# A graph layer on one core: nodes laid 49 to a partition, sources by rounding, the packed list stored in halves

## The chip, the core and the metric

The kernel runs on one core of a Trainium2 chip. The core has TensorE (PE, with PEld for its weight loads), VectorE (DVE), ScalarE (ACT), GpSimd (POOL) and SyncE (SP), each with a queue of its own that it works off in order; 16 DMA engines move data. The metric is the device time of one execution in microseconds, as a median over runs.

## The reference

A graph has 6250 nodes with 64 features and 206250 edges, sorted by their target node `dst`. What is computed:

```python
h = jnp.maximum(_layernorm(x, axis=-1), 0.0)
msg = h[src] + edge_attr_64                      # one row per edge
agg = jax.ops.segment_sum(msg, dst, num_segments=6250)
out = x + (jax.nn.relu(agg @ W1 + b1) @ W2 + b2)
```

W1 is 64x128, W2 is 128x64, all in float32.

## The kernel before

The edges' own rows and the source nodes' rows are summed separately.

Most edges have the sum over `h[src]` done by TensorE as a product. For a window of 252 target nodes a matrix of counts is built (how often does node s send to node d), by comparing lists of keys with ramps (`count`, L704: DVE makes `hot_lo` and `hot_key`, PE multiplies them to `pc`, ACT writes `pc` to `counts`), and then `counts` is multiplied with `h` in three bf16 parts (`product`, L750). There are 310 steps of `count`; a step n has extra work given to it in the dictionary `before` (L894). The edges' own rows come in chunks by SP (`feat`), and are summed against one-hot matrices (`chunk_sum`, L400).

The last 24 groups of 1024 edges (GP) are done otherwise: POOL gathers the source rows from a table of `h` in DRAM and adds them onto the edges' rows in SBUF (`pfeat`, 8 gathers of 128 rows a group, 192 in all), and two groups at a time are summed (`features_h`, L859). When a pair of groups is summed is decided while the program is written out, by a planner that counts 2.2 us a gather and 1.38 us a step.

The order of every engine's work is written by hand (`manual_schedule`). All gathers stand in POOL's queue: `rows` (15), `words` (15 and one for a second list), `dstq` (5) and `pfeat`.

The stretch before step 0, the prologue, does this:

- SP loads `firsts_i` and then x in three thirds of 128 partitions (L151). Node n lies in partition n % 128, so a partition's rows are 256 B runs, 32 KB apart. The last 106 nodes come in a load of their own (L152).
- ACT's queue loads src (L140). ACT turns src to float (L242), and its queue loads dstn, the targets (L243). PE transposes the sources, ACT stores them as `srcl` (`turn_src`, L245).
- From `firsts` DVE and PE find in which row of 256 edges each node's list begins (`row_i`, L259); POOL fetches these rows (`fetch_row`, L275), ACT counts in them where the list begins (`seek`, L279), DVE makes an index of it (`place`, L285).
- DVE packs target and source in one word, (dst << 13) | src (L561), for two halves. One store from ACT's queue writes the list `packed` to DRAM (L564). From there POOL fetches each node's list (`fetch_pair`, L541, tile `words`), and `unpack` and `turn` (L587, L600) make keys of it.
- The layernorm is done by thirds: means (L463), centring and squares (L470, L473), variances (L478), `norm_scale` (L484), and `norm_h` (L492), which stores a third of the table from SP and copies `h` to bf16.
- `chunk_starts`, `chunk_rows`, `chunk_columns`, `chunk_index` (L303 to L339) find where each chunk's edges begin; the gather `dstq` (`fetch_dst`, L344) needs their `cols_i`, and so do the `feat` loads.

Since a node lies at row (n % 128) * 49 + n // 128 of the table, `table_rows` (L521) turns sources into rows by three integer operations, for the `pfeat` gathers.

After the loop come the last two pairs of groups and the rest of the products and the MLP; at step 99 the index of a second, short list is made (`second_n`, L661), for which POOL has one gather of `words`.

Of the kernel before, what the change touches and what calls it, by code (L numbers as in the profile page):

```python
# [9 lines left out]
F32 = mybir.dt.float32  # L10
BF16 = mybir.dt.bfloat16
# [96 lines left out]
def gnn_kernel(ctx: ExitStack, tc: tile.TileContext, x, src_t, dst_t, dst_g, edge, w1, b1, w2, b2, out):  # L108
# [31 lines left out]
    nc.scalar.dma_start(src, src_t[:, :GA * J])  # L140
    dstn = pr.tile([QA, 2, P * J], I32, name="dstn")

    firstp_i = small.tile([1, GP], I32, name="firstp_i")
    nc.scalar.dma_start(firstp_i.rearrange("o (q h k) -> o q h k", h=2, k=1),
                        dst_g[GA // 2:G // 2, :, 0:1].unsqueeze(0))
    xl = consts.tile([P, HI + 1, D], F32, tag="x", name="xl")
    nc.gpsimd.memset(xl[:, HI - 1, :], 0.0)
    thirds = [(0, 16), (16, 32), (32, HI)]
    for h0, h1 in thirds:
        h1 = min(h1, HI - 1)  # L150
        nc.sync.dma_start(xl[:, h0:h1, :], x[h0 * P:h1 * P, :].rearrange("(h l) d -> l h d", l=P))  # L151
    nc.sync.dma_start(xl[:N % P, HI - 1, :], x[N - N % P:, :])  # L152

# [59 lines left out]
    for q in range(JQ):  # L213
# [37 lines left out]
    turn_src(0)  # L251
    pf = ps.tile([P, IC], F32, tag="po", name="pf", bufs=1)
# [22 lines left out]
    def fetch_row(i):  # L275
        rows_of[i] = small.tile([P, L1], I32, name="rows", bufs=4)
        gather(rows_of[i], dst_g.rearrange("q h (r k) -> (q h r) k", k=L1), row_i[:, i:i + 1])

    def seek(i0, n):  # L279
        for i in range(i0, i0 + n):  # L280

            inrow = small.tile([P, L1], BF16, name="inrow", bufs=2)
            nc.scalar.activation(inrow, rows_of[i], AF.Sign, bias=nhalf[:, i:i + 1], accum_out=first[:, i, 1:2])  # L283
# [236 lines left out]

    def table_rows(index, tmp):  # L521

        nc.vector.tensor_scalar(tmp, index, LO_BITS, None, op0=OP.logical_shift_right)
        nc.vector.tensor_scalar(index, index, P - 1, None, op0=OP.bitwise_and)
        nc.vector.scalar_tensor_tensor(index, index, float(HI), tmp, op0=OP.mult, op1=OP.add)

    def find_groups():
# [31 lines left out]
    norm_means()  # L559
    for h in range(2):  # L560
        nc.vector.scalar_tensor_tensor(dstn[:, h], dstn[:, h], DST_BITS,  # L561
                                       srcl[:QA, h].rearrange("q p j -> q (p j)"),
                                       op0=OP.logical_shift_left, op1=OP.bitwise_or)
# [12 lines left out]
    place(3, 4)  # L576
    fetch_pair(2)
    norm_var(2)
# [290 lines left out]
    chunk_starts(0, 2 * RC, "pc", 2)  # L869
    src_hi = late.tile([P, NWIN + NX], BF16, tag="part", name="src_hi").bitcast(I32)[:, :GP * J]  # L870
# [12 lines left out]
    load(1)  # L883
# [7 lines left out]
    def then(k, f):  # L891
# [193 lines left out]
    with tc.If(odd > 0):  # L1085
# [20 lines left out]
        with tc.For_i(0, G, 1) as g:  # L1106
# [6 lines left out]
            nc.sync.dma_start(index, src_t[:, ds(g * J, J)])  # L1113
            index_hi = work.tile([P, J], I32, name="index_hi", bufs=1)
            table_rows(index, index_hi)
            dst_1 = work.tile([P, J], I32, name="dst_1", bufs=1)
# [61 lines left out]
```

## Time and profile before

| | |
|---|---|
| median of 3 runs | 522.75 us (520.2, 522.75, 527.85) |
| profiled execution, its own time | 525.21 us |
| its span, first to last instruction | 523.4 us |
| granted TensorE clock, mean | 0.974 |
| DMA moved | 78.78 MB, 151 GB/s over the span |
| step 0, first count on PE | at 42.9 us |
| first `dstq` gather on POOL | at 37.6 us |
| last `pfeat` gather on POOL | at 503.0 us |

The page gives busy time of each engine, a chain of work that ended last, and groups of instructions by line with what ended the idle time before them. In a timeline the columns are start, duration, engine, line, operation, output<-input, shapes, how many, and in brackets the idle time before it and what ended that. A time of several equal instructions in a row is merged to one line.

### The profile page before, as it was taken

What the parts mean: (1) busy time and instruction counts of PE and PEld (TensorE: products, weight loads), DVE (VectorE), ACT (ScalarE), POOL (GpSimd) and SP (SyncE); (2) the same over time, 40 slices, a digit from 0 to 9 for tenths busy, and PEclk for the clock granted to TensorE, in tenths of its full rate; (3) what the DMA queues carried; (4) which work ended last, traced back from release to release, by engine and by line L of the source; (5) the groups of instructions that cost most, each with busy time, mean ns of one, the idle gap of its engine ahead of it and who ended that gap; (6) DMA issues with size and microseconds to landing.
All of it is one profiled execution on the core that took longest, in us unless ns stands there. A gap on an engine that the chain in (4) does not pass through costs nothing. (4 is left out here: it accounts for less than half of the span.)

```text
span 523.4 us, 19099 instructions
## 1 busy us (share of the span) xinstructions
PE 451.5 (86%) x8183; PEld 385.6 (74%) x8184; DVE 417.4 (80%) x618; ACT 360.1 (69%) x534; POOL 415.7 (79%) x265
## 2 busy tenths in 40 slices
PE   3026767999699999988999999999999999999954
PEld 3015555888588888777888888888888888888743
DVE  5589986889699989988898978888879888879210
ACT  5246898778467767896777777777777777768300
POOL 6358888888888868888889888888888888888840
PEclk9999899999799999999999999999999999999977
DMA  9819812566577766654666676676577676676610
GB/s 203 211 42 329 220 29 39 146 172 156 117 171 179 167 171 181 171 138 95 161 162 155 149 178 153 140 184 163 129 173 175 137 198 146 141 192 164 155 14 14
DMA packets 118152, 78.78 MB, mean 151 GB/s; under 512 B 39096, under 2 KB 113326, under 8 KB 117870
## 3 DMA queue, kind: packets, MB, share of 16 engines
q1 hardware_dynamic: 88458, 64.95, 42.7%
q0 software_dynamic: 29200, 10.25, 16.7%
q10 hardware_dynamic: 404, 2.30, 1.5%
q8 instruction: 66, 1.08, 0.9%
q14 instruction: 24, 0.20, 0.1%
HBM read 73.48 MB, written 3.99 MB: 148 GB/s over the span
## 5 line engine op out<-in xcount | busy, mean ns | idle before, releaser
L267 POOL DMA_INDIRECT pfeat<-table,src_p x192 | 363.5, 1893 | 58.5 <-issue 54.9
L722 ACT ACTIVATE counts<-pc 128x882 bf16<-128x882 f32 x310 | 276.8, 908 | 41.0 <-PE pc L720 27.0
L720 PE MATMUL pc<-hot_key,hot_lo 128*128 128x147 bf16 x1860 | 175.1, 231 | 24.2 <-DVE hot_key L712 17.5
L712 DVE TENSOR_TENSOR hot_lo<-iota_lo,keys 128x1536 bf16<-128x1536 bf16 x155 | 148.0, 955 | 46.5 <-PE pc L720 46.0
L720 PEld LDWEIGHTS <-hot_lo 128*128 128x128 bf16 x1860 | 135.3, 100 | 47.7 <-DVE hot_key L712 22.3
L712 DVE TENSOR_TENSOR hot_key<-iota_key,keys 128x1776 bf16<-128x1776 bf16 x155 | 167.1, 1078 | 0.0
L755 PE MATMUL pv<-counts,h 128*128 128x252 bf16 (+1 forms) x1078 | 149.6, 273 | 0.1
L755 PEld LDWEIGHTS <-h 128*128 128x128 bf16 x1078 | 99.2, 98 | 8.7 <-issue 0.4
L758 PE MATMUL pv<-counts,h 128*64 128x252 bf16 (+1 forms) x1078 | 78.0, 280 | 0.0
L407 PE MATMUL bank<-feat,hot 128*21 128x64 f32 x3168 | 59.0, 223 | 1.5 <-DMA feat<-in_edge 0.8
L410 ACT ACTIVATE by_node<-bank 128x128 f32<-128x128 f32 x66 | 18.4, 278 | 60.8 <-PE bank L407 60.7
L758 PEld LDWEIGHTS <-h 128*64 128x64 bf16 x1078 | 55.3, 113 | 4.4 <-issue 0.8
L407 PEld LDWEIGHTS bank<-feat,hot 128*21 128x21 f32 x3168 | 47.4, 102 | 14.8 <-issue 9.5
L395 DVE TENSOR_TENSOR hot<-rel,iota 128x504 f32<-128x504 bf16 x66 | 44.6, 677 | 0.6 <-PE bank L407 0.6
L267 POOL DMA_INDIRECT rows<-in_dst_g,row_i x15 | 18.6, 1238 | 14.9 <-ACT inrow L283 7.9
L267 POOL DMA_INDIRECT words<-packed,first_i x15 | 19.5, 1302 | 4.6 <-issue 3.4
L419 PE MATMUL pv<-select,by_node 128*64 128x42 f32 x264 | 21.2, 244 | 0.4 <-ACT by_node L410 0.4
L419 PEld LDWEIGHTS pv<-select,by_node 128*64 128x64 f32 x264 | 13.2, 137 | 9.1 <-issue 1.1
L440 PE MATMUL bank<-hotp,pfeat 128*64 128x42 f32 x384 | 14.7, 233 | 5.5 <-DMA pfeat<-table,src_p 4.2
L440 PEld LDWEIGHTS bank<-hotp,pfeat 128*64 128x64 f32 x384 | 12.8, 138 | 8.3 <-DMA pfeat<-table,src_p 4.7
L767 DVE TENSOR_TENSOR sums<-sums,pv 128x252 f32<-128x252 f32 x22 | 9.0, 409 | 10.9 <-PE pv L758 10.9
L309 PE MATMUL pstart<-begins,first 128*1 128x9 f32 (+2 forms) x30 | 1.2, 172 | 19.0 <-DVE first L287 19.0
(171 smaller groups left out, 273.5 us busy)
## 6 DMA issues: line engine op xcount, KB each, us to landing
feat<-in_edge SPq DMA_DIRECT2D x132, 384.0 KB
pfeat<-in_edge SPq DMA_DIRECT2D x24, 256.0 KB
pfeat<-table,src_p POOLq DMA_INDIRECT x192
xl<-in_x SPq DMA_DIRECT2D x3, 512.0 KB
out_y<-y SPq DMA_DIRECT2D x24, 63.0 KB
xs<-in_x SPq DMA_DIRECT2D x4, 315.0 KB
table<-xl SPq DMA_DIRECT2D x2, 512.0 KB
dstn<-in_dst_g ACTq DMA_DIRECT2D x1, 768.0 KB
```

The costliest lines, as they stand in the source:

```text
L267: nc.gpsimd.indirect_dma_start(out=rows, out_offset=None, in_=source, in_offset=bass.IndirectOffsetOnAxis(ap=index, axis=0), compute_op=op)
L395: nc.vector.tensor_tensor(hot_of[u][:, :n].rearrange("p c j w -> p (c j) w"), rel[:, c:c + n].rearrange("p c q k -> p (c q k)").unsqueeze( ...
L407: nc.tensor.matmul(bank[q * QP:q * QP + WQ, i * D:(i + 1) * D], hot[:, i, j, :], feat[i][:, j, :], start=(k == 0), stop=(k == JP - 1))
L410: nc.scalar.activation(by_node[u][:, :n].rearrange("p c d -> p (c d)"), bank[:, :n * D], AF.Copy)
L419: nc.tensor.matmul(pvs[b][0][i * D:(i + 1) * D, a:a + CN], of[:, i, :], select, start=False, stop=False)
L440: nc.tensor.matmul(pa[k:k + D, b, :], tiles[b][:, j, :], hot[:, j, :], start=(j < 2), stop=(j >= J - 2))
L712: nc.vector.tensor_tensor(hot.rearrange("p t (m o) -> p t m o", o=2), iota_k.rearrange("p (m o) -> p m o", o=2).unsqueeze(1).to_broadcast( ...
L720: nc.tensor.matmul(pc[:, k, m * K:(m + 1) * K], hot_lo[:, j, :], hot_key[:, j, :K], start=True, stop=True)
L722: nc.scalar.activation(counts[b % 2][:, :, s * ST * V:(s + 1) * ST * V].rearrange("p h (k m) -> p h k m", k=2), pc[:, :, :ST // 2 * K].rea ...
L755: nc.tensor.matmul(pv, h3[:, h, :2 * D], of, start=(h == 0 and not clear), stop=False)
L758: nc.tensor.matmul(pv[k:k + D, :], h3[:, h, 2 * D:], of, start=False, stop=(h >= HI - 2))
L767: nc.vector.tensor_tensor(at[:, :BN], at[:, :BN], pv[:, o:], op=OP.add)
```

## The change

Node n now lies in partition n // 49, so a partition holds 49 nodes that are neighbours in DRAM, and the table's row of node n is n itself. x comes as 112 partitions in three thirds (runs of 16 or 17 rows of 256 B), 15 partitions whole, and one partition with the last 27 nodes; the places without a node are zeroed first. `table_rows` is gone. The number that is packed for a source still has the partition-wise form, which is now 128 * (s % 49) + s // 49 where before s itself served; so s // 49 is found by scaling, adding and subtracting a large number, and the rest by one combining operation. dstn is loaded behind src at once. Packing is done by halves between the centrings, and each half is stored from SP. Seeks, fetches and places are regrouped: the first pair's words are unpacked after `norm_h`, the rows 7 to 10 are fetched behind `dstq`, and their seeks come at steps 4 and 5 instead of 15 and 16.

```diff
+    nc.scalar.dma_start(dstn, dst_g[:QA])          # behind src's load
...
-    nc.gpsimd.memset(xl[:, HI - 1, :], 0.0)
+    NL = N // HI                                   # 127
     thirds = [(0, 16), (16, 32), (32, HI)]
+    nc.gpsimd.memset(xl[96:, N % HI:, :], 0.0)
     for h0, h1 in thirds:
-        h1 = min(h1, HI - 1)
-        nc.sync.dma_start(xl[:, h0:h1, :], x[h0 * P:h1 * P, :].rearrange("(h l) d -> l h d", l=P))
-    nc.sync.dma_start(xl[:N % P, HI - 1, :], x[N - N % P:, :])
+        nc.sync.dma_start(xl[:112, h0:h1, :], x[:112 * HI, :].rearrange("(l h) d -> l h d", l=112)[:, h0:h1, :])
+    nc.sync.dma_start(xl[112:NL, :HI, :], x[112 * HI:NL * HI, :].rearrange("(l h) d -> l h d", l=NL - 112))
+    nc.sync.dma_start(xl[NL:, :N % HI, :], x[NL * HI:, :].unsqueeze(0))
...
+    lo_f = counts[0].rearrange("p h n -> p (h n)").bitcast(F32)[:, HI * D:HI * D + GA * J]
+    nc.scalar.activation(lo_f, src, AF.Copy, scale=1.0 / HI, bias=-(HI // 2) / HI)
     srcf = src.bitcast(F32)
-    nc.scalar.activation(srcf, src, AF.Copy)
-    nc.scalar.dma_start(dstn, dst_g[:QA])
+    nc.scalar.activation(srcf, src, AF.Copy, scale=float(P))
+    nc.vector.tensor_scalar(lo_f, lo_f, 1.5 * (1 << 23), 1.5 * (1 << 23), op0=OP.add, op1=OP.subtract)
...
-    turn_src(0)                                    # ahead of the products of pf
...
     for i in range(4):
         fetch_row(i)
+    nc.vector.scalar_tensor_tensor(srcf, lo_f, 1.0 - P * HI, srcf, op0=OP.mult, op1=OP.add)
+    turn_src(0)
     turn_src(1)
...
-    for h in range(2):
+    def pack(h):
         nc.vector.scalar_tensor_tensor(dstn[:, h], ...)
-    nc.scalar.dma_start(packed.rearrange("(q k) o -> q (k o)", q=QA), dstn.rearrange("q h k -> q (h k)"))
-    seek(0, 3)
-    for i in range(4, 7):
-        fetch_row(i)
-    place(0, 3)
+        nc.sync.dma_start(packed.rearrange("(q h k) o -> q h (k o)", q=QA, h=2)[:, h], dstn[:, h])
+    pack(0)
+    seek(0, 2)
+    fetch_row(4)
+    fetch_row(5)
+    norm_center(0)
+    pack(1)
+    seek(2, 2)
+    fetch_row(6)
+    norm_center(1)
+    place(0, 2)
     fetch_pair(0)
-    for k in range(3):
-        norm_center(k)
-        if k < 2:
-            seek(3 + 2 * k, 2)
+    norm_center(2)
+    seek(4, 3)
     norm_var(0)
     norm_var(1)
-    place(3, 4)
-    fetch_pair(2)
+    place(2, 5)
     norm_var(2)
...
-    table_rows(src_p, src_hi)
-    unpack_pair(0)
     chunk_rows(0, 2 * RC)
     chunk_columns(0, 2, "pc", 2)
-    turn_pair(0)
     norm_scale()
     chunk_index(0, 2)
     fetch_dst(0)
+    for i in range(7, 11):
+        fetch_row(i)
+    fetch_pair(2)
     fetch_pair(4)
     for k in range(3):
         norm_h(k)
+    unpack_pair(0)
+    turn_pair(0)
...
-        3: [lambda: open_pv(0, True), lambda: rows_later(7, 11)],
-        16: [lambda: seek(9, 2), lambda: rows_later(11, IC)],
-        18: [lambda: place(7, 4)],
+        3: [lambda: open_pv(0, True)],
+        4: [lambda: seek(7, 2)],
+        5: [lambda: seek(9, 2), lambda: rows_later(11, IC)],
+        8: [lambda: place(7, 4)],
-        15: [lambda: seek(7, 2), find_groups, lambda: norm_c(0), lambda: clear(0, 5)],
+        15: [find_groups, lambda: norm_c(0), lambda: clear(0, 5)],
```

The lists that come out differ also in this: with four rows fewer in the planner's queue, the pairs of `pfeat` groups are summed 3 to 6 steps earlier in the loop, the first at step 41 instead of 47; the last two pairs stay behind the loop in both. On POOL 53 `pfeat` gathers now stand ahead of the second list's words, 51 before.

More of the change, by code (lines that the diff above doesn't have):

```diff
@@ L146, in gnn_kernel @@
     xl = consts.tile([P, HI + 1, D], F32, tag="x", name="xl")
-    nc.gpsimd.memset(xl[:, HI - 1, :], 0.0)
+    NL = N // HI
+    assert NL == P - 1
     thirds = [(0, 16), (16, 32), (32, HI)]
+    nc.gpsimd.memset(xl[96:, N % HI:, :], 0.0)
     for h0, h1 in thirds:
-        h1 = min(h1, HI - 1)
-        nc.sync.dma_start(xl[:, h0:h1, :], x[h0 * P:h1 * P, :].rearrange("(h l) d -> l h d", l=P))
-    nc.sync.dma_start(xl[:N % P, HI - 1, :], x[N - N % P:, :])
+        nc.sync.dma_start(xl[:112, h0:h1, :], x[:112 * HI, :].rearrange("(l h) d -> l h d", l=112)[:, h0:h1, :])
+    nc.sync.dma_start(xl[112:NL, :HI, :], x[112 * HI:NL * HI, :].rearrange("(l h) d -> l h d", l=NL - 112))
+    nc.sync.dma_start(xl[NL:, :N % HI, :], x[NL * HI:, :].unsqueeze(0))
     zero = small.tile([P, 1], F32, name="zero")
@@ L519, in gnn_kernel @@
     nc.sync.dma_start(dst_p, dst_t.rearrange("p (g j) -> p g j", j=J)[:, GA:, :])
[L521 to L525, printed above, removed]
     def find_groups():
@@ L869, in gnn_kernel @@
     chunk_starts(0, 2 * RC, "pc", 2)
-    src_hi = late.tile([P, NWIN + NX], BF16, tag="part", name="src_hi").bitcast(I32)[:, :GP * J]
-    table_rows(src_p, src_hi)
-    unpack_pair(0)
     chunk_rows(0, 2 * RC)
     chunk_columns(0, 2, "pc", 2)
-    turn_pair(0)
     norm_scale()
@@ L1113, in gnn_kernel @@
             nc.sync.dma_start(index, src_t[:, ds(g * J, J)])
-            index_hi = work.tile([P, J], I32, name="index_hi", bufs=1)
-            table_rows(index, index_hi)
             dst_1 = work.tile([P, J], I32, name="dst_1", bufs=1)
```

## The prediction

> **What bounds the kernel now.** I read the page's busy shares first, then the chain that ended last in order of time, then the waits of POOL, and then the timelines of the two places these point to: the prologue and the neighbourhood of 190 us.
>
> ```profile
> PE 451.5 (86%) x8183; PEld 385.6 (74%) x8184; DVE 417.4 (80%) x618; ACT 360.1 (69%) x534; POOL 415.7 (79%) x265
> ```
>
> No engine is full, so the share decides nothing. The chain at the end does:
>
> ```profile
> 501.17 1.55 POOL pfeat L267
> 502.72 0.30 issue
> 503.03 3.56 DMA pfeat<-table,src_p
> 506.59 0.04 issue
> 506.63 0.45 PE bank L440 x2
> ```
>
> PE stands idle for the last `pfeat` gathers of POOL. By the timeline the last pair of groups (L440) would have been summed at about 501.9 with its data there, and was at 507.07: 5.2 us of slack on PE. What sets POOL's end? Its waits:
>
> ```profile
> POOL pfeat L267 <- issue: 54.9, 180, 0.3
> POOL rows L267 <- ACT inrow L283: 7.9, 1, 7.9
> POOL dstq L267 <- DVE cols L339: 4.5, 1, 4.5
> POOL words L267 <- DVE second_n L661: 3.8, 1, 3.8
> POOL rows L267 <- DVE row_i L259: 3.1, 1, 3.1
> ```
>
> The reader is to see that from the `dstq` gather on POOL waits for others only once, 3.85 us for `second_n`, a result of the counting loop. All else is 0.3 us between one gather and the next. POOL's end is therefore the start of `dstq`, plus a fixed list of gathers, plus that one wait. The prologue that leads to `dstq`, and to the loop:
>
> ```profile
> 19.09 2.35 DVE L561 SCALAR_TENSOR_TENSOR dstn<-dstn,srcl 96x1024 int32<-96x1024 int32 x2
> 21.85 0.51 ACT L283 ACTIVATE inrow<-rows,nhalf 128x256 bf16<-128x256 int32 x1 [8.80 <-DVE dstn L561]
> 22.71 0.95 POOL L267 DMA_INDIRECT rows<-in_dst_g,row_i  x1 [7.90 <-ACT inrow L283]
> 23.97 1.80 POOL L267 DMA_INDIRECT rows<-in_dst_g,row_i  x1 [0.30 <-issue]
> 26.07 2.04 POOL L267 DMA_INDIRECT rows<-in_dst_g,row_i  x1 [0.31 <-ACT counts L473]
> 28.42 0.95 POOL L267 DMA_INDIRECT words<-packed,first_i  x1 [0.30 <-DVE stat L478]
> 30.01 0.51 ACT L283 ACTIVATE inrow<-rows,nhalf 128x256 bf16<-128x256 int32 x1 [1.54 <-DMA rows<-in_dst_g,row_i]
> 37.64 1.82 POOL L267 DMA_INDIRECT dstq<-in_dst_g,cols_i  x1 [4.53 <-DVE cols L339]
> ```
>
> The chain: the last third of x is used at 17.67, after 2.71 us of waiting; then `pack` on DVE; the store of `packed` stands in ACT's queue, so ACT idles 8.80 us until the pack is done before it can seek; rows 4 to 6 are fetched only then; their last seek at 30.01 leads to `cols` and `dstq`. The loop's first count follows at 42.89.
>
> **The change, part by part.**
>
> *Loads.* src, dstn and x are 0.73 + 0.79 + 1.60 = 3.12 MB. x now comes in runs of 4 KB where it came in 256 B. The DMA view of the first 20 us, in half microseconds, shows both kinds:
>
> ```profile
> GB/s 0 0 0 68 57 171 376 433 331 94 264 225 216 218 216 368 211 287 236 270 237 202 157 189 219 216 219 217 218 237 261 321 282 332 108 107 191 296 270 188
> ```
>
> From 3 to 4.5 us, with src's 5.6 KB runs in flight, 331 to 433; later, mostly short runs, some 215. From 2.3 us on, 3.12 MB end at 10.5 (at 380) or at 16.8 (at 215). The new runs are nearer to the first row, so I take 12. SP's issue of the three thirds (6.22 us before, 5.14 more for the remainder) falls away; the five loads need no more than the table stores' 0.33 us each. The longer zeroing of `xl` on POOL (1472 columns; 0.15 us for 64 and 0.21 for 128 make 1.5) lies in POOL's 3.1 us wait for `row_i`; without that cover it would cost 1.5.
>
> *Sources by rounding.* ACT converts twice, 1.39 us each (L242): from 5.2 to 8.0. DVE rounds 128x1424: bounds 0.87 (the slope from 15 columns, 0.17 us, to 256, 0.29) and 1.69 (L561's kind, 1.22 for 1024); I take 0.9, the same operation's row. It lies in DVE's 0.98 us wait for `pf`; without it `row_i` is late by as much. If src lands later than 6.8, the rounding holds `row_i` up too; rows 0 and 1 are needed at 18 and land near 14, so some 3 us are covered. Then on the path: the combining operation, 1.69, from 9.9 to 11.6; three small ones to 12.2; the reductions 1.22 + 1.22 + 1.29 and L466 to 16.2. Meanwhile PE turns (2.0 each) from 11.6, and ACT stores `srcl` (2.1 each) at 15.7 and 17.8, `row2` at 18.0. `firstp_i` stands behind dstn now and must land by 11.6; it is 0.1 KB.
>
> *Packing in halves, stores on SP.* DVE: pack, center, pack, center (1.22 each) to 21.0, place 0.35, center, two variances to 24.9. ACT is free at 18.0, not at 21.85: seeks 0 and 1 to 19.0, square, seeks 2 and 3 to 21.1, squares to 23.7. POOL: row 4 at 18.6, 5 at 20.7, 6 at 22.8. Both first ones are beside DVE operations of two inputs, so 1.8 us each as at 23.97, not 0.95; row 6 lands at 25.7 (before, 28.11 to 30.01). Seek 6 and place end at 26.7, the last variance at 28.0. From L481 to `dstq` were 4.68 us; `table_rows` (0.86) and the unpacking (0.87) are gone from them: 2.95. **`dstq` starts at 31.0, 6.6 us earlier.** The halves' store, issued at 19.8, must land by then less two gathers; before it took at most 6.9 us (21.48 to 28.42), which would be 26.7 and still covered. On SP the first half's store waits for pack 0 (17.4), the second for pack 1 (19.8). Behind them stand two `pfeat` loads, not touched until about 47, and the table's stores, not ready before 32; so nothing on SP is late. Moving dstn's load to the front costs ACT 0.34 us of issue before src has landed.
>
> The rows' new place costs: gathers took 1.80 and 2.04 us beside L470, 0.95 beside the reductions. The sum has the slow ones; with 0.95 throughout, `dstq` would come 1.3 us earlier. The Trainium skill (SBUF — State Buffer, "Who interferes with whom") has a rule that speaks against this place: a DVE operation with two SBUF inputs contends with GpSimd instructions that read SBUF, a reduction on this chip never does; by it the sum is the one made here, without it the gain would be 1.3 us more.
>
> *POOL's list.* Two words gathers move from the idle prologue behind `dstq`, and four rows come under the norm_h operations. Bounds: 2 x 1.25 = 2.5 to 2 x 2.33 = 4.7 (the slowest words row, 2.03 + 0.3); I take 3.2, since some of them run clear. Besides, 53 instead of 51 `pfeat` gathers (2.2 us with its gap) stand ahead of the `second_n` words, so 2 fewer follow. POOL arrives there at 187.9 - 6.6 + 3.2 + 4.4 = 188.9.
>
> ```profile
> 191.74 0.90 POOL L267 DMA_INDIRECT words<-packed,second_i  x1 [3.85 <-DVE second_n L661]
> ```
>
> If the loop gains 2.9 us or more by then, nothing is waited for: POOL ends 6.6 - 3.2 + 3.85 = **7.25 us earlier**.
>
> *The loop.* The unpacking and turning of pair 0 come after norm_h. norm_h ends at 34.3, ACT's three h copies at 35.4, `klo` 0.42, transposes 1.1, keys 1.0, two hot operations 2.0: first count at 40.0, so 2.8 us earlier, and the 0.47 us wait for `dstq` goes. Unpacking used to be hidden; now DVE is idle about 2.8 us before the loop. Four seeks move from steps 15 and 16 to 4 and 5:
>
> ```profile
> 44.00:48.00 4.00, 2.94 (x20) 2.21 (x19) 4.00 (x5) 2.65 (x4) 3.39 (x3) 1.00 0.96 290
> ...
> 64.00:68.00 4.00, 2.64 (x28) 2.10 (x28) 3.38 (x4) 4.00 (x8) 3.69 (x2) 1.00 0.30 55
> ```
>
> Columns: stretch, its length, busy PE, PEld, DVE, ACT, POOL, clock. At 64 ACT is full (4.00 of 4), at 44 it is not (2.65) and DVE is. The seeks took 0.99 + 0.98 us there, so 0 to 2.0; I take 1.2. The loop gains 2.8 + 0.4 + 1.2 = 4.4, above the 2.9 needed. PE could end 4.4 + 5.2 = 9.6 us earlier, more than POOL's 7.25, so POOL decides.
>
> *The sum.* The profiled execution took 525.2 (span 523.4, 1.8 around it): 525.2 - 7.25 = 518.0. It lies 2.5 above the median of the runs shown, 522.75; on that footing 515.5. With x landing at 16.8, `dstq` starts 4.4 later and the gain is 2.85: 519.9. With fast gathers (6.6 + 1.3 - 2.5 + 3.85) it is 9.25: 513.5.
>
> **The rivals.** *The loop doesn't start earlier.* If the keys come late, behind norm_h and the copies, the loop keeps its 42.89, and `second_n` its 191.4. POOL then gains only the two gathers that no longer follow, 4.4 us: 518.4. For it: DVE idles before the loop. Against: 2.8 us of margin.
>
> *The tail of x.* Partitions 112 to 127 come in two loads of 15 and 1 long rows, and the first reduction waits for both besides its own third. At a sixteenth of 380 GB/s, 195 KB take 8.2 us; begun at 12, they end at 20.2, so the reductions start 7.9 late and `dstq` at 38.9, 1.3 later than now. With 3.2 more on POOL and 3.85 absorbed the end is 0.65 later: 523.4, slower. It decides from a first reduction later than 12.3 + 7.25 = 19.5. For it: no row here shows so few long rows. Against: 15 rows are not one.
>
> *More than the sum.* If the gathers at the loop's start also run clear of the burst at 40 to 52 us (290 to 379 GB/s in the windows), and of DVE, POOL's seven gathers from 37.64 to 50.0 fall from 1.46 to 0.95 each, 3.6 more, and the seeks give all 2.0: PE's 9.6 + 0.8 then decides, 512.3. For it: rows and words did go in 0.95 where they ran alone. Against: DVE has no pause there.
>
> **How the numbers follow.** Forecast 0.57 (513.5 to 519.9), loop or less than intended 0.18, tail 0.09, more 0.16. Time 515.5; 512.0 to 522.0 leaves out most of the tail and the far side of the last case. 2% is about what a measurement of this kernel can tell from no change, 10.5 us. Faster by that: half of the last case, which lies on the bound, and, since the three runs shown spread from 520.2 to 527.85, a quarter of the forecast: 0.08 + 0.16 = 0.24. Slower by that needs a tail far worse than priced: 0.05.
>
> **What would show it.** In the profile of after: the first `stat<-xl` reduction near 12.3; ACT without the 8.8 us wait; `dstq` near 31; the first count near 40; no wait at the second words; POOL's last gather near 497, PE still waiting briefly for it. A first reduction after 17, a count after 42, or a POOL wait that is new between 50 and 500 would make the prediction wrong.

## The result, and the profile after

The changed kernel takes 538.7 us (median of 4 runs, 537.42 to 539.5), the kernel before 524.16 beside it: a ratio of 1.028, with a 95% interval of 1.0228 to 1.0331. It is slower, where 515.5 and no measurable change were forecast. The profiled execution took 538.0 (span 536.1), against 525.21 (span 523.4). The granted TensorE clock, 0.934 in it against 0.974 before, does not explain this: two of the four runs had 0.96 and took 539.4 and 539.5.

The shares of the page have hardly moved. POOL has 13 us more than before, in as many instructions:

```profile
PE 452.4 (84%) x8183; PEld 386.4 (72%) x8184; DVE 417.8 (78%) x617; ACT 361.0 (67%) x535; POOL 428.9 (80%) x265
```

The chain that ended last (start, duration, what) still runs over POOL's last gathers; the last of them starts at 516.63, 13.6 us later than before (503.03):

```profile
514.77 1.55 POOL pfeat L274
516.32 0.30 issue
516.63 3.69 DMA pfeat<-table,src_p
```

POOL's waits (total, times, longest) show what moved:

```profile
POOL dstq L274 <- DVE cols L346: 6.5, 1, 6.5
POOL words L274 <- DVE second_n L669: 5.9, 1, 5.9
POOL rows L274 <- DVE nhalf L271: 5.2, 1, 5.2
...
POOL rows L274 <- ACT inrow L290: 2.2, 2, 1.9
```

The 7.9 us wait for the seek is gone as intended, but the waits for the row numbers (3.1 before), for `cols` (4.5) and for `second_n` (3.8) have each grown by about 2 us. Some rows of the prologue from the timeline, each with its start, its duration and the idle time before it:

```profile
9.35 0.17 DVE L232 CAST firsts<-firsts_i 128x8 f32<-128x8 int32 x1 [5.50 <-DMA firsts_i<-in_dst_g]
16.97 3.54 DVE L470 TENSOR_REDUCE stat<-xl 128x16 f32<-128x1024 f32 x3 [1.75 <-DMA xl<-in_x]
20.63 0.51 ACT L290 ACTIVATE inrow<-rows,nhalf 128x256 bf16<-128x256 int32 x1
21.49 3.46 POOL L274 DMA_INDIRECT rows<-in_dst_g,row_i  x1 [1.94 <-ACT inrow L290]
31.45 0.51 ACT L290 ACTIVATE inrow<-rows,nhalf 128x256 bf16<-128x256 int32 x1 [0.64 <-DMA rows<-in_dst_g,row_i]
36.63 1.82 POOL L274 DMA_INDIRECT dstq<-in_dst_g,cols_i  x1 [6.50 <-DVE cols L346]
```

x is there at 16.97, the last seek runs at 31.45, and `dstq` starts 1.0 us earlier than before, not 6.6. The rate of the DMA in the first 20 us, in half microseconds, says why x is late: 365 to 410 GB/s only from 3 to 4.5 us, then 330 and 295 and after that mostly 230 to 285.

```profile
GB/s 0 0 0 80 80 216 365 410 375 330 295 230 279 246 174 141 255 238 270 270 262 239 263 285 244 343 265 88 59 48 48 33 9 252 45 80 138 316 242 139
```

POOL's rows near 65 us hold the longest gather of the run. It is one of the four `rows` gathers of the last slabs, which took 0.94 to 1.54 us before:

```profile
64.87 1.54 POOL L274 DMA_INDIRECT rows<-in_dst_g,row_i  x1 [0.30 <-issue]
66.71 9.50 POOL L274 DMA_INDIRECT rows<-in_dst_g,row_i  x1 [0.30 <-issue]
76.52 1.65 POOL L274 DMA_INDIRECT pfeat<-table,src_p  x1 [0.30 <-issue]
```

And at step 62 of the loop, rows of three engines, the chunk's numbers that `chunk_nodes(1)` reads (L359) are not there:

```profile
140.94 0.95 POOL L274 DMA_INDIRECT dstq<-in_dst_g,cols_i  x1 [0.30 <-issue]
...
144.11 0.42 DVE L359 TENSOR_SCALAR dstq<-dstq,cols 128x384 f32<-128x384 int32 x1 [11.70 <-DMA dstq<-in_dst_g,cols_i]
...
147.10 0.92 PE L728 MATMUL pc<-hot_key,hot_lo 128*128 128x147 bf16 x6 [12.83 <-DVE hot_key L720]
```

VectorE stands 11.7 us for a gather that POOL reaches only at 140.94, and PE stands behind VectorE. The same gather and the same operation of VectorE in the kernel before:

```profile
130.06 1.53 POOL L267 DMA_INDIRECT dstq<-in_dst_g,cols_i  x1 [0.30 <-issue]
134.23 0.42 DVE L352 TENSOR_SCALAR dstq<-dstq,cols 128x384 f32<-128x384 int32 x1 [1.98 <-DMA dstq<-in_dst_g,cols_i]
```

The second list's words come at 203.01, and now after a longer wait than before (3.85):

```profile
203.01 0.90 POOL L274 DMA_INDIRECT words<-packed,second_i  x1 [5.92 <-DVE second_n L669]
```

### The profile page after: what moved, and what is told of

Same layout as the page of the kernel before. It is cut to its first block, busy times and chain, and to the rows that moved or that the text cites. A ratio compares the mean times of both kernels' runs of the same rounds, so it can differ in the third digit from the quotient of the medians.

```text
span 536.1 us, 19097 instructions
## 1 busy us (share of the span) xinstructions
PE 452.4 (84%) x8183; PEld 386.4 (72%) x8184; DVE 417.8 (78%) x617; ACT 361.0 (67%) x535; POOL 428.9 (80%) x265
## 5 line engine op out<-in xcount | busy, mean ns | idle before, releaser
L763 PE MATMUL pv<-counts,h 128*128 128x252 bf16 (+1 forms) x1078 | 152.2, 276 | 0.1
L763 PEld LDWEIGHTS <-h 128*128 128x128 bf16 x1078 | 100.7, 99 | 9.5 <-issue 0.4
L414 PE MATMUL bank<-feat,hot 128*21 128x64 f32 x3168 | 57.9, 221 | 1.7 <-DVE hot L402 0.8
L274 POOL DMA_INDIRECT rows<-in_dst_g,row_i x15 | 29.3, 1955 | 11.2 <-DVE nhalf L271 5.2
L274 POOL DMA_INDIRECT words<-packed,first_i x15 | 18.3, 1221 | 4.7 <-issue 3.4
L819 PE MATMUL ph<-sums,w1s 128*128 128x252 f32 (+1 forms) x50 | 15.8, 399 | 1.5 <-DVE sums L436 0.9
```

What stands on the lines that cost most here:

```text
L274: nc.gpsimd.indirect_dma_start(out=rows, out_offset=None, in_=source, in_offset=bass.IndirectOffsetOnAxis(ap=index, axis=0), compute_op=op)
L414: nc.tensor.matmul(bank[q * QP:q * QP + WQ, i * D:(i + 1) * D], hot[:, i, j, :], feat[i][:, j, :], start=(k == 0), stop=(k == JP - 1))
L763: nc.tensor.matmul(pv, h3[:, h, :2 * D], of, start=(h == 0 and not clear), stop=False)
L819: nc.tensor.matmul(ph[:, :n], w1s, agg[:, start[b]:start[b + 1]], start=True, stop=True)
```

## The experiments

The 18 kernels ran in five groups, on several chips. The kernel before ran beside each group and took 522.0, 535.8, 523.4, 537.0 and 534.9, so across groups only ratios to it can be set side by side, and these with care: where it took 535 or more, the loop came later to the same places (`second_n` at 192.75 in b5_dst1_dstn, by 188.98 in b3_dst1_early), and in several kernels POOL then waited 5 to 12 us for `second_n` although its list had become shorter. The ratios of a1_dst1_early, a2_seeks_late, a3_dstn_late, a7_pause_once and a9_words_first have intervals that overlap with the changed kernel's own (1.0228 to 1.0331), so what a single edit gives is read from the place of POOL's last gather in one profiled execution of each, not from its time.

### First group: three suspects, each taken back alone

**a1_dst1_early**, the changed kernel with the second chunk's gather ten steps earlier in POOL's list:

```
-        before.setdefault(n, []).append(lambda t=t: queue.insert(0, (GATHER_US, lambda: fetch_dst(t))))
+        before.setdefault(n - (10 if t == 1 else 0), []).append(lambda t=t: queue.insert(0, (GATHER_US, ...
```

> The changed kernel with one edit: the gather of the second chunk's dst numbers (fetch_dst(1)) is put at the head of POOL's list ten steps earlier. Theory (the loop waits for POOL): in the changed kernel this gather starts at 140.9 and VectorE stands 11.7 us at L359 for it, then second_n comes at 203.0 and POOL waits 5.9 us for it. With the gather ten steps (some 20 us) earlier the 11.7 us wait is gone or under 1 us, second_n is ready near 192, POOL reaches its words at about 197 without a wait, and the end comes 5.9 us earlier: 532 (530 to 534). Rival (the late prologue alone sets the end, the stall is cover): nothing moves by more than 2 us, 536 to 540. Rival (the stall is all of the loss): 524 to 527.

Measured: 531.6 (before 522.0; ratio 1.0216, 1.0146 to 1.0286). The gather starts at 127.77, VectorE does not wait for it, and the second list's words follow without a wait:

```profile
197.80 0.90 POOL L274 DMA_INDIRECT words<-packed,second_i  x1 [0.30 <-issue]
```

The last gather starts at 510.70, 5.93 earlier than in the changed kernel: just the wait for `second_n` that went, as the first theory had it. The loop did find a new wait, 7.24 us for the third chunk at 170.66, but with nothing of POOL waiting for its results it cost nothing.

**a2_seeks_late**, the changed kernel with the seeks and their place back where they were:

```
-        4: [lambda: seek(7, 2)],
-        5: [lambda: seek(9, 2), lambda: rows_later(11, IC)],
-        8: [lambda: place(7, 4)],
+        16: [lambda: seek(9, 2), lambda: rows_later(11, IC)],
+        18: [lambda: place(7, 4)],
...
-        15: [find_groups, ...
+        15: [lambda: seek(7, 2), find_groups, ...
```

> The changed kernel with one edit: the seeks of slabs 7 to 10, their place and the rows behind them go back to steps 15, 16 and 18, where they stood before. Theory (a gather is held up while VectorE runs two-input operations without a pause): the gather that took 9.5 us at 66.7 meets a pause of VectorE again near step 18 and takes 5 us or less; fetch_dst(1) starts about 5 us earlier (near 136), VectorE's 11.7 us wait falls to 5 to 8, and the time to 531 to 534. Rival (the long gather has to do with what POOL or the DMA queues carry): a gather of 8 us or more stays in the first 100 us, and the time stays at 536 to 540.

Measured: 533.3 (ratio 1.0206, 1.0131 to 1.0282). `place` again waits 1.07 us for its seek near 70, VectorE pauses, and the long gather, now a `pfeat`, takes 4.18 us. `fetch_dst(1)` starts at 134.07 (136 expected) and VectorE's wait is 6.44. The rest is in the first theory's ranges. Of the 6.9 us by which that gather is earlier, 3.3 reach the end (last gather at 513.36), since POOL's wait for `second_n` grew to 7.51. But with the edit the order of the gathers had changed too, so whether the pause or the order did it was open.

**a3_dstn_late**, the changed kernel with dstn's load behind ACT's conversions:

```
     nc.scalar.dma_start(src, src_t[:, :GA * J])
-    nc.scalar.dma_start(dstn, dst_g[:QA])
...
     nc.scalar.activation(srcf, src, AF.Copy, scale=float(P))
+    nc.scalar.dma_start(dstn, dst_g[:QA])
```

> The changed kernel with dstn's load back behind ACT's two conversions. Theory (the 1024 four-byte pieces of firsts_i share the DMA engines with dstn's long runs): firsts_i lands at 5.8 again, not 9.35, row_i is at about 9.5, not 12.7. What it gives at the end: the seeks are at 20.6 for other reasons (first reduction at 17.0), so dstq comes 0 to 1.5 earlier and the time is 536 to 538. Rival A (row_i's 3.3 us are the prologue's loss): dstq at 33.3 and 533 to 535. Rival B (firsts_i is late for x's long runs): firsts_i stays near 9 and nothing moves.

Measured: 533.9 (ratio 1.0215, 1.0149 to 1.0281). `firsts_i` is used at 5.82 and `row_i` is there at 9.20, as expected, but the forecast for the end missed: dstq came 3.45 earlier. What the forecast had not seen is that x comes earlier by as much:

```profile
13.66 3.54 DVE L470 TENSOR_REDUCE stat<-xl 128x16 f32<-128x1024 f32 x3 [1.83 <-DMA xl<-in_x]
...
33.18 1.81 POOL L274 DMA_INDIRECT dstq<-in_dst_g,cols_i  x1 [6.38 <-DVE cols L346]
```

By an estimate, dstn's 0.79 MB take some 2.9 us at the 270 GB/s of these microseconds, and in the changed kernel x pays them. The number was rival A's, but the run does not separate `row_i` from x. The seeks stand behind two things that end together in the changed kernel: x's reductions (until 20.51) and ACT's stores of `srcl` (until 20.80), whose combining operation VectorE runs behind `row_i`'s. With dstn late both come earlier, the reductions by 3.31 us and the stores, which begin at 13.52 instead of 16.92, by 3.40.

**b1_dstn_early**, the mirror of it: the kernel before with that one load at the front.

> The kernel before with dstn's load right behind src's on ACT's queue, as in the changed kernel, and nothing else. Theory: firsts_i lands at about 9.3 where it landed at 5.8, row_i at 12.7; ACT's 8.8 us wait for the pack covers most of it, so dstq moves by 0 to 1 us and the time is 523 to 526. Rival (x's long runs hold firsts_i up): firsts_i stays at 5.8 and the time is that of before. Rival (the late row_i is what costs): dstq 3 us later, 527 to 529.

Measured: 519.9 (ratio 0.9962, 0.9928 to 0.9996), `firsts_i` used at 9.54 and `row_i` there at 12.83, as the first theory said; its time, 523 to 526, was too high. The late `row_i` costs nothing there: ACT's wait covers it (4.48 us of the 8.80 are left), and `dstq` even comes 0.9 earlier (36.74), since the last third of x, whose short runs SyncE issues until 13.1 anyway, is used at 16.79 (17.67 before). The same edit costs 3.5 us in one kernel and nothing in the other, because in the changed one nothing is left between the seeks and the two things that the load delays.

### Second group: what holds a gather up, and where x's tail lands

The kernel before took 535.8 beside this group.

**a5_light_once**, one VectorE operation more at step 17:

```
+        nc.vector.tensor_scalar(spare[:, :n], iota_q[:, :n], 1.0, None, op0=OP.mult)    # n = 256
...
-        17: [lambda: norm_c(1), ...
+        17: [lambda: light(2 * P), lambda: norm_c(1), ...
```

> The changed kernel with one VectorE operation more: at step 17, ahead of the second norm_c, a TENSOR_SCALAR of one input (128x256, result not used). Work is added, none removed. Theory (a gather is held up as long as VectorE runs two-input operations without a pause): the gather that starts at 66.7 ends about 1.4 us after this operation, near 70.5, so it takes 3 to 4 us and not 9.5; all that follows on POOL is 5 to 6 us earlier, fetch_dst(1) at 135, the wait at L359 6 to 7 us, and the time comes to 532 to 534 (like the kernel with the seeks late). Rival (the gather is long for what POOL or the DMA queues hold at that moment, and the late seeks helped by the order of the gathers): it stays at 9 us or more, time 536 to 540. Rival (it needs a real pause of VectorE): the same as that.

The theory failed. The operation stands where it was meant to, at 68.59 (0.27 us), and the gather stays as long as it was:

```profile
66.44 9.71 POOL L274 DMA_INDIRECT rows<-in_dst_g,row_i  x1 [0.30 <-issue]
```

Its four runs spread from 539 to 553 (the profile is of one of 550), so nothing is read from its time.

**b2_light_each**, the kernel before with such an operation (128x128) behind each pair of hot operations:

```
                     keys[:, k, t:t + 2 * ST, :].unsqueeze(2).to_broadcast([P, 2 * ST, m, 2]), op=OP.is_equal)
+            light(P)
```

> The kernel before with one VectorE operation more behind each pair of hot operations: a TENSOR_SCALAR of one input (128x128, about 0.17 us, result not used), some 165 of them, 28 us of work added to VectorE. Theory (gathers that meet two-input operations back to back wait for the next one-input operation or pause): no gather is over 3.0 us any more, where five were from 3.0 to 5.4 us; POOL's list gets 5 to 20 us shorter and PE's slack of 5 us at the end is used up: 515 to 520 beside 522 for before. Rival (VectorE has no room for 28 us): the counts come later in the stretches where VectorE is full, and the time is 524 or more.

Measured: 535.7, ratio 1.0005 (0.9967 to 1.0043). Gathers of 4.46, 6.36 and 3.46 us are still there: against the theory too. So such an operation, 128 or 256 columns wide, does not reliably let a gather through; what kinds do is taken up in the last section.

**a4_tail_first**: dstn late, and x's two tail loads ahead of its thirds.

```
+    nc.sync.dma_start(xl[112:NL, :HI, :], ...
+    nc.sync.dma_start(xl[NL:, :N % HI, :], ...
     for h0, h1 in thirds:
         nc.sync.dma_start(xl[:112, h0:h1, :], ...
```

> The changed kernel with dstn's load behind ACT's two conversions (as in a3_dstn_late) and the two loads of x's last 16 partitions ahead of its thirds. With dstn late alone the thirds landed at 8.2, 9.9 and 12.7 and the 15-partition load at 13.6, where the first reduction began. Theory (the tail load holds the reductions up by the little it lands behind the last third): the reductions begin at 11.4, behind the combining operation, and end at 15.0 to 16.3; ACT's seeks still wait for its copies of srcl until 18.0, so dstq comes 0 to 1.9 earlier than 33.2 and the time is 532 to 534. Rival (the load of 15 long rows is slow by itself, 8 us or so): the first reduction still waits for it until 12 or later, and nothing moves.

The first reduction starts at 12.01 with no wait for x, and `dstq` at 32.30, 0.9 earlier than in a3_dstn_late: inside the first theory's range. Here the reductions are 1.65 earlier and ACT's stores of `srcl` are not (13.79), so in this prologue the stores hold the seeks. SyncE's later issues wait in order for its earlier loads; read so, the 15-partition load landed by 7.4 here, and with the thirds ahead of it 0.9 behind the last of them (13.55 after 12.67). It is not slow by itself. The runs spread from 534 to 548 (ratio 1.0002, 0.9949 to 1.0055; the profile is of one of 548), so only its prologue is used.

**a6_dst1_dstn**: the edits of a1_dst1_early and a3_dstn_late together.

> The changed kernel with two edits together: fetch_dst(1) ten steps earlier (alone 531.6) and dstn's load late (alone 533.9). Theory (POOL's list from the first dstq gather on sets the end, and the two edits act at different places of it): dstq starts at 33 and POOL waits for nothing from there on, so the gains add: last gather near 507, time 528 (526 to 530). Rival (a new wait of the loop or of POOL takes part of it, for the loop stands 7 us for the third chunk's dst numbers already): 531 or more.

Measured: ratio 1.009 (1.0044 to 1.0137; the 528 expected would be 1.011 of the 522.0 it was made from). Last gather at 511.06 with the 9.50 us gather still in it, and POOL waits 1.3 us for `second_n` and 5.9 behind 400 us, for PE and a load. So the gains add nearly, and here the loop begins to share the end.

### Third group: a pause, the three together, the list

The kernel before took 523.4.

**a7_pause_once**: at the same place as a5_light_once, three operations on one column, each reading the one before.

```
+        for k in range(3):
+            nc.vector.tensor_scalar(spare[:, k + 1:k + 2], (spare[:, k:k + 1] if k else iota[:, 0:1]), 1.0, ...
...
+        17: [rest_a_moment, lambda: norm_c(1), ...
```

> The changed kernel with a short real pause of VectorE at step 17, ahead of the second norm_c: three operations on one column, each reading what the one before wrote, so that VectorE has to run empty in between. Theory (a gather is held up as long as VectorE's operations follow each other without a gap, and is through about 1.4 us after the first gap; a single independent operation left none): the gather that starts near 66.7 ends near 70.5 and takes 3 to 4 us, not 9.5; the wait at L359 falls to 6 to 7 us, and the time falls by 3 to 6 us against the changed kernel, to a ratio of 1.017 to 1.023 to the kernel before. Rival (it has to do with POOL or the DMA queues): it stays at 9 us or more, ratio 1.028.

Measured: 532.9, ratio 1.0171 (1.0091 to 1.0251). VectorE's rows, and POOL's:

```profile
67.27 1.06 DVE L725 TENSOR_TENSOR hot_key<-iota_key,keys 128x1776 bf16<-128x1776 bf16 x1
68.26 0.13 DVE L713 TENSOR_SCALAR spare<-iota 128x1 f32<-128x1 f32 x1
68.43 0.34 DVE L713 TENSOR_SCALAR spare<-spare 128x1 f32<-128x1 f32 x2
68.69 1.22 DVE L512 TENSOR_TENSOR h<-xl,h 128x1024 bf16<-128x1024 f32 x1
```

```profile
66.11 3.04 POOL L274 DMA_INDIRECT rows<-in_dst_g,row_i  x1 [0.30 <-issue]
```

The first operation ends at 68.39 and the next begins at 68.43: here alone an operation of VectorE starts after the one before has ended, not some 0.1 us ahead of that. The gather that took 9.50 us is through at 69.15. Half a microsecond of work added takes 6.5 us out of this gather, with the gathers in the same order, so the order is not it; `fetch_dst(1)` starts at 133.93 instead of 140.94. POOL then waits 7.52 us for `second_n`, and the last gather is 5.35 earlier (511.28). That the 0.04 us gap did it was the theory; the last section shows that it did not need the gap.

**a8_three**: the edits of a1_dst1_early, a2_seeks_late and a3_dstn_late together.

> The changed kernel with three edits together: fetch_dst(1) ten steps earlier, dstn's load late, the seeks of slabs 7 to 10 late. Theory (three losses at different places of one list: 3.5 us of late loads, 5.3 us of a held-up gather, 5.9 us of waiting for second_n; 14.7 together, the whole of the loss): last gather at 502 to 504, time that of the kernel before, ratio 0.995 to 1.005. Rival (they overlap, or another wait takes their place): ratio 1.01 or more.

Measured: 523.3 against 523.4, ratio 0.998 (0.9944 to 1.0016). `dstq` at 33.76, no wait of POOL over 0.6 us behind it, and the end where it was before (503.03):

```profile
503.13 1.55 POOL L274 DMA_INDIRECT pfeat<-table,src_p  x1 [0.30 <-issue]
```

The three account for the whole loss against the kernel before. The 7.25 us that were forecast beyond that are still missing: `dstq` comes 2.8 later than the 31.0 of the sum, the list to the second words is 1.7 shorter than forecast, and the stretch behind them is 1.9 us longer than before (313.19 for 311.29) where 4.4 less was forecast.

**a9_words_first**: the changed kernel with `fetch_pair(2)` ahead of `fetch_dst(0)` on POOL.

> The changed kernel with fetch_pair(2) ahead of fetch_dst(0) on POOL, as before the change: two words gathers then stand in POOL's idle 6.5 us at 30 to 36.6. Theory (POOL's list from dstq on sets the end; two gathers of 1.6 us and their gaps leave it): dstq stays at 36.6, fetch_dst(1) and all behind it come 3.8 us earlier, ratio to before 1.019 to 1.022 (3 to 4 us off the changed kernel). Rival (dstq is put off by the words, or the loop sets the end): less than 1.5 us, ratio 1.025 or more.

Measured: 535.4, ratio 1.0239 (1.0188 to 1.029). `dstq` is at 36.45 as before, so the two gathers (0.94 each at 32.55 and 33.79) are free there; the last gather comes 3.05 earlier. That is less than the 3.8 expected: the held-up gather, now a `pfeat`, begins at 65.33 and takes 11.11, ending at the same VectorE operations as before.

**b3_dst1_early**: the kernel before with `fetch_dst(1)` ten steps earlier.

> The kernel before with fetch_dst(1) ten steps earlier. In its profile VectorE waits 1.98 us for that gather and POOL later 3.85 us for second_n. Theory (the loop's wait for this gather comes back to POOL through second_n): VectorE's wait is gone, second_n comes 2 us earlier, POOL's wait falls to about 1.9, and the time is 1 to 3 us shorter, ratio 0.994 to 0.998. Rival (the wait is hidden, or the gather ahead of others delays words that the keys need): ratio 1.0 or more.

Measured: 521.8, ratio 0.9992 (0.9958 to 1.0026): too small to be told from nothing in time. In the trace it is as expected: VectorE's wait of 1.98 is gone, the second list's words come at 188.98 without a wait (191.74 after 3.85), the last gather at 500.68 (503.03).

### Fourth and fifth group: what is left

The kernel before took 537.0 beside the first four and 534.9 beside the last two. The pause is here two dependent one-column operations (about 0.3 us) behind every third pair of hot operations:

```
+            if (b * STEPS + s) % 6 == 0:
+                rest_a_moment()
```

**a10_words_first3**, a8_three with `fetch_pair(2)` ahead of `fetch_dst(0)`:

> The changed kernel with the three edits (fetch_dst(1) early, dstn late, seeks late: level with before at 0.998) and fetch_pair(2) ahead of fetch_dst(0). Theory (POOL's list behind dstq is still what ends last; two words gathers leave it): last gather at about 499.5 where it was 503.1, time 3 to 4 us less, ratio 0.990 to 0.993. Rival (PE has no slack): ratio 0.996 or more.

**a11_pauses3**, a8_three with the pauses:

> The changed kernel with the three edits and two dependent one-column operations of VectorE behind every third pair of hot operations (0.3 us each time, some 55 times, 16 us of work added). Theory (gathers over 2.6 us are held up for want of a pause): none over about 4 us is left (5.0, 7.0 and 5.4 us before), POOL's list gets some 8 to 12 us shorter, until PE's own work ends last: ratio 0.985 to 0.993. Rival (VectorE is too full, or the gathers are as long in sum): ratio 0.998 or more.

**a12_all**, both, and the tail loads first:

> The changed kernel with the three edits, fetch_pair(2) ahead of fetch_dst(0), the two tail loads of x ahead of its thirds, and the pauses. Theory (POOL stops being the bound, PE's last work ends the kernel): the last pfeat gather ends 10 us or more before the end of the others' waits, time 512 to 518, ratio 0.98 to 0.99. Rival (the loop is slower for the pauses): 0.993 or more.

Measured: ratios 1.0034 (1.0 to 1.0067), 1.0084 (1.0049 to 1.012) and 0.9995 (0.9957 to 1.0033). The rivals' side all three times. In all three POOL now waits for the loop: 6.3, 9.6 and 7.9 us for `second_n`, and further waits of 2 to 6 us behind 320 us for PE or a load. A shorter list can give nothing there; what it would give where the kernel before takes 523 was not measured. The pauses did what was expected of them on the gathers: behind 205 us the longest is 3.67 us in a11_pauses3, where a8_three has 7.00 and 5.38.

**b4_pauses**, the kernel before with `fetch_dst(1)` early, dstn's load early and the pauses, and **b5_dst1_dstn**, the same without the pauses:

> The kernel before with fetch_dst(1) early, dstn's load early (alone 0.996) and the same pauses. Theory: five gathers of 3.0 to 5.4 us fall below 3, POOL's list is 5 to 8 us shorter, and the time 515 to 519, ratio 0.985 to 0.992. Rival (PE's slack of 5 us is less than that or VectorE too full): ratio 0.995 or more.

> The kernel before with fetch_dst(1) early and dstn's load early, without pauses. If the pauses carried the 0.992 of the kernel that has them too: 0.996 to 1.0. If the two early steps carried it: 0.990 to 0.994.

Measured: b4_pauses 531.9 against 537.0, ratio 0.9924 (0.9885 to 0.9962), the lowest ratio of all, though by less than 2%; b5_dst1_dstn 533.1 against 534.9, ratio 0.9984 (0.995 to 1.0018). So the pauses seem to carry most of it; the intervals overlap, and gathers of 4.31, 5.38 and 3.19 us were still there with them, so this is not shown.

**a13_pauses_alone**, the changed kernel, nothing undone, with the pauses, the first at step 16 (the remainder 4 instead of 0):

> The changed kernel with nothing undone, and two dependent one-column operations of VectorE behind every third pair of hot operations, the first of them at step 16. Theory (held-up gathers cost the changed kernel 5.3 us at 66.7 and 6.4 us after second_n): the 9.5 us gather falls to 4 or less, those of 5.1, 7.0 and 5.4 us behind 200 us to 3 or less, and the last gather comes 7 to 11 us earlier: ratio to before 1.007 to 1.015 beside 1.028. Rival (the pauses only move the hold-ups, or VectorE's 16 us of added work take the gain): 1.02 or more.

Measured: 538.5 against 534.9, ratio 1.0094 (1.0067 to 1.0121), inside the range. The 9.5 us gather takes 4.03, VectorE's wait at L359 falls from 11.70 to 0.77, and POOL does not wait for `second_n`. Gathers of 6.26 and 5.06 us are still there at 148.5 and 204.7, but behind them the longest is 3.16. The last gather is at 512.92, 3.7 us earlier than in the changed kernel and not the 7 to 11 expected, and behind 330 us POOL has new waits of 1.2 to 5.5 us for PE and for loads. The comparison with 1.028 is across chips, so its size is only roughly known.

## Why the prediction was wrong

The sum can be taken apart at the same points in both traces. POOL's last gather was to come 7.25 us earlier and came 13.60 later, 20.85 apart:

| POOL | predicted | measured | off by | where the number is from |
|---|---|---|---|---|
| start of `dstq` | -6.6 | -1.01 | 5.6 | 37.64 to 36.63 |
| list from there to the second words | +7.6 | +10.21 | 2.6 | 150.25 to 160.46, without the wait |
| wait for `second_n` | -3.85 | +2.07 | 5.9 | 3.85 to 5.92 |
| list from there to the last gather | -4.4 | +2.33 | 6.7 | 311.29 to 313.62 |

**The loads.** The term "I take 12" for x was mis-sized: 16.97, the far end of its own bounds (16.8). The row read for long runs, 331 to 433, was three half microseconds with src in flight; x's 4 KB runs, with dstn late, came at some 275 GB/s (short ones at 217). And dstn in front makes x and `firsts_i` wait 3.3 to 3.6 us. The prediction named the move's cost as 0.34 us of issue; with dstn back, `dstq` is at 33.2. It also took for granted that `row_i` stays at 9.4; it came at 12.71, and with it the combining operation at 13.13 for 9.9, so ACT's stores of `srcl` ended at 20.80 and not at 17.8. The rounding itself was right (0.90, hidden), and the combining operation took 1.62 for 1.69.

**The rows' new place.** The first row gather beside pack and center took 3.46 us for 1.8, the next two 0.95 and 1.04 for 1.8 and 0.95. With dstn late, `dstq` stays 2.2 us short of 31.0: 1.4 of it is x (13.66 for 12.3), and the rest lies between, where the last three seeks wait 1.25, 0.78 and 0.21 us for their rows.

**"POOL waits for others only once."** True of POOL, and the wrong question. The loop waits for POOL: VectorE stood 1.98 us at L352 for the second chunk's numbers before the change already, in the waits of VectorE, which were not read. The loop reached that place at 132.41 (132.25 before), although its first count was 2.8 us late and not 2.8 early, and then stood until 144. So `second_n`, which was to be ready in time, is ready 11.3 us later than before, and POOL waits for its own lateness. a1_dst1_early took 5.93 out of the end by moving one gather, and b3_dst1_early shows the same circle, 2 us wide, in the kernel before. Where two engines wait for each other, neither's list can be summed alone.

**POOL's list.** Two words gathers and two `pfeat` ahead of the second words were counted about right: a8_three, without the gather of 9.50 us, has 156.2 us there, 5.9 more than before, for 7.6. What was missing is the gather of 9.50. The seeks' move was priced as ACT's time alone, as a gain of 1.2 us for the loop. But it also took away VectorE's only pause in a stretch that is otherwise full, 1.34 us at L287, and that pause was what let the gather at 64.62 through in 4.18:

```profile
64.62 4.18 POOL L267 DMA_INDIRECT pfeat<-table,src_p  x1 [0.30 <-issue]
...
66.18 1.21 DVE L505 TENSOR_TENSOR h<-xl,h 128x1024 bf16<-128x1024 f32 x1
68.72 0.17 DVE L287 SCALAR_TENSOR_TENSOR first<-first,middle 128x4 f32<-128x4 f32 x1 [1.34 <-ACT inrow L283]
```

This is a wait turned into a gain for one engine and a loss for another.

**The tail of the list.** Two fewer gathers follow, 4.4 us less, and the stretch grew: those of 5.07, 3.87, 7.00 and 5.38 us make 21.3, where before four made 14.9 (3.04, 3.32, 5.38, 3.19). The same gathers meet the same VectorE operations at another phase. The prediction took the mean gap-and-gather of 2.2 us as fixed. a11_pauses3 and a13_pauses_alone shorten just these.

**The rivals.** The tail of x stays out: those partitions land 1.1 us behind the last third (16.87 after 15.79 by SyncE's waits), not 8.2. The loop did start later than forecast (45.68), but this rival's price does not hold either, since the second chunk's wait swallowed it. "More than the sum" had its reason, gathers that run clear of VectorE, on the right engine and with the wrong sign.

**What was to show it.** Two signs were well chosen: the first reduction, at 16.97, stood at its limit of 17, and the first count, at 45.68, was past its limit of 42. The last, a new wait between 50 and 500, was looked for on POOL; it came on VectorE.

## What to carry to other kernels

Read the waits of every engine on the list you sum, and of the engines that read its results: a 2 us wait of the other side is a closed circle, in which each delay goes round. A load moved to the front was paid here by whatever had become first on the path, so ask what lands later, not what the issue costs. A wait of one engine can be another engine's only opening; before filling it, look at what ends behind it.

## What the runs showed of the hardware

An indirect gather of POOL can be held up while VectorE runs operations with two inputs from SBUF one behind the other. The traces date the moment when it gets in. A `pfeat` gather that is not held takes about 1.55 us and a `rows` gather 0.95. In the 20 traces 95 gathers took over 3 us, and every one of them is through 1.42 us (`pfeat`) or 0.82 us (`rows`) after the end of one of VectorE's operations, to 0.04 us; any other moment would lie as near to such an end in about one case of eleven. So a held gather behaves as if it stood still near its start until an operation of VectorE ends, and then took its usual time.

What follows on VectorE at that end is, in 47 cases, a gap, such as the one at 67.38 in the kernel before (68.80 is 1.42 later). In 38 it is, without any gap, an operation that reads at most one tensor from SBUF, one of a single column or with its other input from PSUM, for instance. In the changed kernel `hotp` ends at 251.62, and the gather at 253.04; `pv` lies in PSUM:

```profile
249.17 3.87 POOL L274 DMA_INDIRECT pfeat<-table,src_p  x1 [0.31 <-issue]
...
250.71 0.91 DVE L443 TENSOR_TENSOR hotp<-dst_p,iota 128x336 f32<-128x336 f32 x2
251.54 0.40 DVE L775 TENSOR_TENSOR sums<-sums,pv 128x252 f32<-128x252 f32 x1
251.87 0.94 DVE L720 TENSOR_TENSOR hot_lo<-iota_lo,keys 128x1536 bf16<-128x1536 bf16 x1
```

In the other 10 an operation with two inputs follows, so some gathers do get in between two of these. In a7_pause_once the gather is through 0.82 us after `hot_key` ends at 68.33: it got in at the first one-column operation, ahead of the gap at 68.39. For the gather of 9.50 us the opening came here, at the end of `khi` (75.40, and 76.21 is 0.81 later):

```profile
73.92 1.06 DVE L720 TENSOR_TENSOR hot_key<-iota_key,keys 128x1776 bf16<-128x1776 bf16 x1
74.91 0.27 DVE L599 TENSOR_SCALAR klo<-words 128x256 int32<-128x256 int32 x1
75.12 0.28 DVE L600 TENSOR_SCALAR khi<-words 128x258 int32<-128x258 int32 x1
75.43 0.43 DVE L604 TENSOR_TENSOR khif<-khi,nbase 128x258 f32<-128x258 int32 x1
```

`klo` and `khi` have one input each and did not let it in, no more than the operation of a5_light_once, which is of their kind and size. The Trainium skill (SBUF — State Buffer, "Who interferes with whom") says that the pair of ports shared by VectorE and GpSimd is locked for a whole instruction, and that an instruction with at most one SBUF input keeps out of it only outside the two-port modes, which `tensor_scalar` can enter. The traces fit both halves. An operation that reads one tensor from SBUF opens the way, and a wide `tensor_scalar` need not; that these ran in such a mode is an estimate from their pace, 0.27 us for 256 columns and 0.13 for one, about half the time per column of `h<-xl,h` (1.21 for 1024). The section does not say how often a gather can lose: held for one instruction the gather of 9.50 us would have waited 1.3 us at most, and ten of VectorE's operations went ahead of it one by one. It is not known why VectorE wins so often, nor why most gathers get through a full VectorE in 1.5 us: the one at 63.04 did, between operations of the same kind.

A load of 1024 four-byte pieces, 4 KB in all, was used at 5.8 us where src and x were loading beside it, and at 9.4 to 9.5 with 0.79 MB of long runs issued behind src on another queue, in both kernels.
